# A short first chunk, its pool opened beside the image stage, residuals moved to another queue and stored in one transfer

## The chip, the cores and the metric

The kernel runs on one core of a Trainium2 chip. The core has four compute engines, TensorE (PE), VectorE (DVE), ScalarE (ACT) and GpSimd (POOL), and SyncE (SP), whose queue here only starts transfers. ACT and POOL have queues of their own from which transfers can start as well. All engines run their instructions in order and wait for one another by semaphores. The metric is the time of one execution on the device, in microseconds (us); three executions of the kernel before took 2004.09, 2007.87 and 2011.77, median 2007.87.

## The reference

The input is four images of 56 x 56 positions and 128 channels. Two layers follow each other, all in float32:

```python
# layer 0: neighbourhood attention (7x7, 4 heads), then a dense block
x = x + proj(attend(qkv(layernorm(x))))
x = x + fc2(gelu(fc1(layernorm(x))))
# layer 1, on tokens t (4, 3136, 128)
t = t + linear_attention(layernorm(t))        # q * sum_n(k * v)
t = t + stu_mixture(layernorm(t))
# stu_mixture, for each of the leading T, T/2, T/4, T/8 tokens:
#   sum over 16 filters k: irfft(rfft(phi[:, k]) * rfft(u)) @ (sigma[k]**.25 * M_phi_plus[k])
#   + the same with alternating signs and M_phi_minus
#   + three lags: u shifted by 0, 1, 2 tokens @ M_u[i]
# the mixture weights are a straight-through one-hot over the four lengths
```

The last line, the spectral filters, is the larger part of the second half of the kernel. In the frequency domain each bin has its own 128 x 128 complex matrix, made of the filters' values at this bin and of the matrices M.

## The kernel before, in words

**Image stage.** The images b = 0 to 3 are worked on one after another, each in seven groups (g) of 8 image rows = 448 tokens. An image's residual stream x lies in one of two places in SBUF, so image b + 2 is fetched into the place of image b (`fetch`, L97, on SP). For each image there is the attention (softmax on DVE, ACT and POOL: `lows`, `exps`, `shares`; L763, L777, L790), and the rest as a generator, `finish_image` (L511): the dense block, the linear attention, and the preparation of the filters. The attention of image b + 1 and `finish_image` of image b are woven together; each `yield` hands over its estimate of PE time. The whole stage, called the front, is written in manual order: every engine runs its instructions as the program text emits them. That ends with `front.close()`, which also gives the front's SBUF and PSUM space back; after it a scheduler orders the instructions.

In `finish_image` the transforms come first. For each of four slices j of the tokens, `px` (L698) multiplies tables `tab`, fetched on SP (L298), with transposed tokens `tok` (copied from PSUM by ACT, L694). The results are added by DVE and POOL into `ab`, and POOL's queue stores them as `ud[j, b]` (L722). In the last image, which has the extra pool `own`, j = 0 and 2 use `ab` and j = 1 and 3 the second buffer `ab2`.

Then, or between the slices for images 0 to 2, `last_steps` (L666) goes over the groups. `recent(g)` computes the three lags on PE (`par`, L640), and DVE adds them to x in place (L648). `residual(g - 1)` transposes the sum in four pieces on PE (`pf`, L656), ACT copies it (`xf`, L659), and SP stores it in DRAM as `xd` with four transfers, one per piece of 112 tokens, in runs of 512 B (L662). For images 0 and 1 the fetch of the same group of image b + 2 follows on SP. In images 0 to 2 xf has two buffers; in the last image it shares three buffers with `tok`.

**Matrices.** Along with the last image's `finish_image`, `matrices` (L997 to L1019) loads the M matrices on SP and combines them on DVE into `mc`. One of its steps is run for each 1 / 0.4 of yielded PE time.

**Chunk stage.** There are 245 bins, in 31 chunks (c) of 8, the last with 5. For each chunk, `tokens` fetches the spectra of all images and slices from `ud` (`xc`, L1048, 1 MB), and combines them into `v` (`evens`, L310 to L317, on POOL, for chunk 0 on DVE; `odds`, L321 to L330, and three more instructions, L1060 to L1062, on POOL). Both need scratch, `ev` and `od`, which share one buffer. `filters_of` loads `ph` for four chunks (L1070). `make(c, u)`, u = 0 to 7, computes the bins' matrices in 16 matmuls (`pg`, L1084), and DVE and ACT copy them, two copies each of 128 x 512, into `g` (L1097, L1095), which has two buffers. `product(c, part)`, eight parts, multiplies g with v (`py`, L1115); ACT and DVE combine the sums (`ya` L1128, `ys` L1132), and SP stores them in `yd` (L1134). The chunk loop runs make(c + 1, u) and product(c, u) alternately; before it, chunk 0 is made alone. All of the chunk stage's pools open after `front.close()`. For chunk 0, ph and xc are fetched on POOL's queue.

**Back transform.** After the last chunk, `ring` tiles take the sums back from `yd` in 8 transfers per parity and half on SP (`fetch_back`, L1151); butterflies on DVE (L1193, L1194) and matmuls with the table `io` (fetched on ACT, L1159) follow (`pi`, L1232); the residual xd is loaded again and added (L1244), and the result stored (L1248).

`busy(n)` issues n small matmuls whose result nobody reads.

Of the kernel before, what the change touches and what calls it, by code (L numbers as in the profile page):

```python
# [9 lines left out]
FP = mybir.dt.float32  # L10
# [15 lines left out]
GT = GR * W  # L26
QC = 14
# [22 lines left out]
NCH = -(-R // FC)  # L50
FB = 4
# [7 lines left out]
def conv_attn_hybrid_kernel(ctx: ExitStack, tc: tile.TileContext, a: dict, out: bass.AP):  # L59
# [17 lines left out]
    order = tc.manual_schedule()  # L77
    front.enter_context(order)
# [432 lines left out]
    def finish_image(b, own=None):  # L511
# [118 lines left out]
        for r in range(2):  # L630
            spread(r, f"u{b}", rs, scale)
            yield 0.25
        def recent(g):
# [3 lines left out]
            for c0, c1 in zip(cuts, cuts[1:]):  # L637
# [9 lines left out]
            xg = raster(x[:, g])  # L647
            nc.vector.tensor_tensor(  # L648
                xg, ps[:, :GT].rearrange("c (h t w) -> c h t w", h=GR, t=NQ), xg, ALU.add
            )  # L650

        def residual(g):

            pf = ps_s.tile([TQ, NQ, C], FP, tag="s", name=f"pf_{b}_{g}")
            for t in range(NQ):
                nc.tensor.transpose(pf[:, t, :], x[:, g, t * TQ : (t + 1) * TQ], ident)  # L656
            tag, bufs = ("tok", 3) if own else ("xf", 2)
            xf = fp.tile([TQ, NQ, C], FP, tag=tag, name=f"xf_{b}_{g}", bufs=bufs)
            nc.scalar.copy(xf, pf)  # L659
            rows_of = xd[b].rearrange("(g h t w) c -> g t h w c", g=NG, h=GR, t=NQ)  # L660
            for t in range(NQ):
                nc.sync.dma_start(rows_of[g, t], xf[:, t, :])  # L662
            if b + 2 < B:
                fetch(b + 2, [g])
# [12 lines left out]
        abs_of = (ab, own.tile([C, NCH, PH, 2 * FC], FP, name="ab2") if own else ab)  # L677
# [48 lines left out]
        if b == B - 1:  # L726
            yield from last_steps(range(NG))
# [265 lines left out]
    weighed = ExitStack()  # L993
    mpool = weighed.enter_context(tc.tile_pool(name="matrices", bufs=1, side="right"))
# [25 lines left out]

    with tc.tile_pool(name="last", bufs=1, side="right") as own, tc.tile_pool(
        name="weigh", bufs=1, side="right"
    ) as wp:
        extra, due = matrices(wp), 0.0
        for spent in finish_image(B - 1, own):
            due += 0.4 * (spent if spent != "step" else 0.5)
            while due >= 1:
                next(extra, None)
                due -= 1
        run(extra)  # L1030
    front.close()

    gpool = ctx.enter_context(tc.tile_pool(name="wg", bufs=2))
    with tc.tile_pool(name="w3", bufs=2) as wp, tc.tile_pool(
        name="ps_g", bufs=6, space=PSUM
    ) as ps_g, tc.tile_pool(name="ps_y", bufs=2, space=PSUM) as ps_y:
        filters_in, made, spectra, sums = {}, {}, {}, {}  # L1040
        many = [min(FC, R - FC * c) for c in range(NCH)]

        def tokens(c):


            n = NP * B
            x = wp.tile([C, n, CW], FP, tag="xc", name=f"xc{c}")
            (nc.sync if c else nc.gpsimd).dma_start(  # L1048
                x, ud.rearrange("j b c w -> c (j b) w")[:, :, CW * c : CW * (c + 1)]
            )  # L1050
            y = x.rearrange("c n (p r f) -> c p r n f", r=2, f=FC)
            v = wp.tile([C, 3, n * FC, PH], FP, tag="v", name=f"v{c}")
            w = v[:, 1:].rearrange("c r k m -> c m r k")
            gp = nc.gpsimd
            ev = wp.tile([C, 4, 2, n, FC], FP, tag="od", name=f"ev{c}", bufs=1)
            evens(gp if c else nc.vector, ev, y[:, :4], w[:, :4])
            od = wp.tile([C, 3, 2, 2, n, FC], FP, tag="od", name=f"od{c}", bufs=1)
            odds(gp, od, y[:, 4:])
            od = od.rearrange("c i p r n f -> c i p r (n f)")
            gp.tensor_tensor(w[:, 4:6], od[:, 0], od[:, 2], ALU.add)  # L1060
            gp.tensor_tensor(w[:, 6:], od[:, 0], od[:, 2], ALU.subtract)
            gp.tensor_scalar(v[:, 0], v[:, 2], -1.0, 1.0, ALU.mult, ALU.mult)  # L1062
            spectra[c] = v

        def filters_of(k):

            t = wp.tile([C, FB * CW], FP, tag="ph", name=f"ph{k}")
            n = min(FB, NCH - FB * k) * CW
            for rg in range(4):
                (nc.scalar if k else nc.gpsimd).dma_start(  # L1070
                    t[32 * rg : 32 * rg + 32, :n], pd[:, FB * CW * k : FB * CW * k + n]
                )
            filters_in[k] = t

        def make(c, u):

            if u == 0:
                made[c] = gpool.tile([C, CW, C], FP, tag="g", name=f"g{c}")
            g, t, at = made[c], filters_in[c // FB], c % FB * CW
            banks = [ps_g.tile([C, 4, CW], FP, tag="g", name=f"pg_{c}_{u}_{i}") for i in range(4)]  # L1080
            for q in range(4):
                for rg in range(4):
                    r = slice(32 * rg, 32 * rg + 32)
                    nc.tensor.matmul(  # L1084
                        banks[rg][:, q, :],
                        mc[r, 4 * u + q, :],
                        t[r, at : at + CW],
                        start=True,
                        stop=True,
                    )  # L1090
            for rg in range(4):
                into = g[:, :, 32 * rg + 4 * u : 32 * rg + 4 * u + 4]
                src = banks[rg].rearrange("c q n -> c n q")
                if rg % 2:
                    nc.scalar.copy(into, src)  # L1095
                else:
                    nc.vector.tensor_copy(into, src)  # L1097

        def weights(v, r, f, m):

            return v[:, r : r + 2].rearrange("c r (n f) m -> c f m (r n)", f=FC)[:, f, m]

        def product(c, part):

            v, g = spectra[c], made[c]
            f0 = part // 4 * 4
            h, last = part // 2 % 2, min(many[c], f0 + 4)
            if part % 2 == 0:
                sums[0] = ps_y.tile([C, 4, C], FP, tag="y", name=f"py_{c}_{part}")
            py, f1 = sums[0], f0 + part % 2 * 2  # L1110
            for f in range(f1, min(f1 + 2, last)):
                for r in range(2):
                    for m in range(4):
                        slot = SLOTS.index(4 * h + m)
                        nc.tensor.matmul(  # L1115
                            py[32 * m : 32 * m + 32, f - f0, :],
                            weights(v, 1 - r, f, slot),
                            g[:, (2 * slot + r) * FC + f, :],
                            start=(r == 0),
                            stop=(r == 1),  # L1120
                        )
            if part % 2 == 0:
                return

            k = last - f0
            if h == 0:
                sums[1] = wp.tile([C, 4, C], FP, tag="ya", name=f"ya_{c}_{part}", bufs=1)
                nc.scalar.copy(sums[1][:, :k], py[:, :k])  # L1128
                return
            for i, op in enumerate((ALU.add, ALU.subtract)):  # L1130
                ys = wp.tile([C, 4, C], FP, tag=f"ys{i}", name=f"ys_{c}_{part}_{i}")
                nc.vector.tensor_tensor(ys[:, :k], sums[1][:, :k], py[:, :k], op)  # L1132
                at = FC * c + f0
                nc.sync.dma_start(yd[i, at : at + k, :C].rearrange("f q e -> q f e"), ys[:, :k])  # L1134

        ring, ready, waves_back = [], {}, {}
        PAIR = 2 * B * C

        def ring_tile():
            name = f"ring{len(ring)}"
            ring.append(gpool.tile([C, 2, 4, 2, PAIR], FP, tag="g", name=name))

        def fetch_back(pair, par, fh):
            y = ring[fh][:, 1 - par]

            for m in range(4):
                for r in range(2):
                    row = 16 * (2 * m + r) + 8 * pair  # L1150
                    nc.sync.dma_start(  # L1151
                        y[:, m, r],
                        yd[par, RT[fh] : RT[fh] + C, row : row + 8].rearrange("f n e -> f (n e)"),
                    )
            return y.rearrange("f m s (j x) -> f j m s x", j=2)

        def odd_waves(pool, pair, fh):
            t = pool.tile([C, 32 * L], FP, tag="io", name=f"io_{pair}_{fh}")
            nc.scalar.dma_start(t, a["itab_odd"][pair, fh])  # L1159
            return t.rearrange("f (j k m r p n) -> f j k m r p n", j=2, k=2, m=2, r=2, p=2)  # L1160

        filters_of(0)
# [257 lines left out]
```

## Time and profile before

| | |
|---|---|
| median of three executions | 2007.87 us |
| profiled execution | 2007.11 us, of which span 2005.3 |
| PE busy, mean granted clock | 1870.1 us (93%), 0.96 |
| DVE, ACT, POOL busy | 1201.7, 1029.5, 904.8 us |
| image stage up to the last slices | 0 to 1083 us |
| last image's dense block and transforms | 1083 to 1241 us |
| passage to the chunks | 1241 to 1287 us |
| chunk loop | 1287 to 1803 us |
| back transform | 1803 to 2005 us |
| mean DMA rate over the span | 110 GB/s of HBM traffic |

In the lines of the profile, L1084 is line 1084 of the kernel before, `pg<-ph,mc` means that pg is written from ph and mc, and `A <- B: 9.2, 6, 2.9` that instruction group A waited 9.2 us in total for B, 6 times, longest 2.9. In the table of stages the columns are: stretch and its length, busy time (and number of instructions) of PE, of PE's weight loads, of DVE, ACT and POOL, then PE's granted clock as a share of full speed, the busy share of the 16 DMA engines, and GB/s. In the chain, every line is a start, a duration and the work that held up the next. SPq is the time that SP's queue took to issue a transfer. A name with DMA in front is a transfer's time after its issue.

### The profile page before, as it was taken

How to read it: one execution, taken by the hardware profiler on the slowest of the kernel's cores; microseconds unless marked ns; L12 is line 12 of the kernel's file. 1: busy time of each engine (PE TensorE's matmuls, PEld its weight loads, DVE VectorE, ACT ScalarE, POOL GpSimd, SP SyncE). 2: the span in 40 equal slices, each digit the busy share in tenths (PEclk: the TensorE clock that was granted, in tenths of full speed). 3: DMA queues.
4: the chain of work that ended last, by engine and by line, in shares of the span. 5: the costliest groups of instructions: out<-in, count | busy, mean ns of one | idle time of the engine just before them, and what ended most of it. 6: DMA issues, size and time to landing. Idle time of an engine off the chain costs nothing.

```text
span 2005.3 us, 57209 instructions
## 1 busy us (share of the span) xinstructions
PE 1870.1 (93%) x23914; PEld 1196.6 (60%) x23914; DVE 1201.7 (60%) x2749; ACT 1029.5 (51%) x2311; POOL 904.8 (45%) x1446
## 2 busy tenths in 40 slices
PE   6899999998999998999998989799999999996998
PEld 3555555554555554555555445688888888882333
DVE  2676645454645554545556674577777777775883
ACT  1566685654685654685655433355555555550000
POOL 2344322464321563322564026588877777770000
PEclk8799999898999998999999989799999999997999
DMA  4040000053000063000154538444444444439991
GB/s 114 31 133 12 1 1 1 28 197 129 1 1 1 28 212 113 1 1 1 54 184 158 181 96 280 112 135 130 134 130 125 119 130 133 128 88 373 369 329 65
DMA packets 191391, 223.45 MB, mean 111 GB/s; under 512 B 12008, under 2 KB 171049, under 8 KB 188540
## 3 DMA queue, kind: packets, MB, share of 16 engines
q1 hardware_dynamic: 182992, 166.69, 27.1%
q0 software_dynamic: 2752, 34.33, 4.4%
q10 hardware_dynamic: 5388, 18.76, 2.6%
q8 instruction: 189, 3.10, 0.6%
q14 instruction: 70, 0.57, 0.1%
HBM read 141.77 MB, written 77.97 MB: 110 GB/s over the span
## 4 chain that ended last, share of the span: by engine, by line
PE 74%; issue 7%; DVE 5%; DMA 5%; ACT 4%; POOL 2%; SPq 2%; ACTq 0%; DVEq 0%; POOLq 0%
PE pg L1084 14%; PE py L1115 13%; PE pi L1232 7%; PE px L698 4%; PE ppt L806 4%; PE pl L750 3%; PE ph L549 3%; PE pf L540 3%; PE par L640 2%; PE pav L863 2%; PE pv L826 2%; DMA ring<-yd 2%; PE pk L481 2%; SPq L662 2%; DVE p L763 1%
## 5 line engine op out<-in xcount | busy, mean ns | idle before, releaser
L790 POOL TENSOR_SCALAR p<-p,den 112x280 f32<-112x280 f32 x448 | 216.1, 502 | 497.7 <-DVE den L788 265.5
L1097 DVE COPY g<-pg 128x512 f32<-128x512 f32 x496 | 319.8, 688 | 156.4 <-PE pg L1084 147.4
L1095 ACT COPY g<-pg 128x512 f32<-128x512 f32 x496 | 271.1, 602 | 234.1 <-PE pg L1084 226.7
L1084 PE MATMUL pg<-ph,mc 32*128 32x128 f32 x7936 | 297.0, 286 | 10.7 <-ACT g L1095 4.1
L1084 PEld LDWEIGHTS pg<-ph,mc 32*128 32x128 f32 x7936 | 249.7, 189 | 51.1 <-issue 39.1
L777 ACT ACTIVATE p<-p,low 112x280 f32<-112x280 f32 x448 | 231.1, 517 | 93.8 <-DVE low L763 93.5
L1115 PE MATMUL py<-g,v 128*32 128x128 f32 x7840 | 274.8, 281 | 2.6 <-issue 1.1
L1115 PEld LDWEIGHTS py<-g,v 128*32 128x32 f32 x7840 | 218.8, 152 | 32.2 <-issue 3.2
L763 DVE CUSTOM_DVE_ANT_0 p<-pl,bias 112x280 f32<-112x280 f32 x448 | 174.7, 445 | 15.6 <-PE pl L750 3.5
L698 PE MATMUL px<-tab,tok 98*128 98x496 f32 x256 | 122.0, 618 | 18.4 <-DMA tab<-in_tab 9.2
L813 DVE COPY pt<-ppt 120x448 f32<-120x448 f32 x112 | 69.4, 620 | 110.8 <-PE ppt L806 109.9
L806 PEld LDWEIGHTS ppt<-ident,p 112*120 112x120 f32 x896 | 100.4, 139 | 58.0 <-issue 41.5
L806 PE MATMUL ppt<-ident,p 112*120 112x112 f32 x896 | 127.0, 263 | 5.2 <-DVE middle L848 3.9
L1232 PE MATMUL pi<-ring,io 128*98 128x512 f32 x256 | 113.2, 603 | 17.2 <-DVE ring L1194 16.2
L706 POOL TENSOR_TENSOR ab<-ab,w 128x496 f32<-128x496 f32 x60 | 74.1, 1235 | 104.6 <-ACT w L705 87.0
L813 ACT COPY pt<-ppt 120x448 f32<-120x448 f32 x224 | 87.2, 444 | 53.9 <-PE ppt L806 53.6
L750 PE MATMUL pl<-kt,qt 32*112 32x280 f32 x896 | 94.8, 442 | 11.5 <-ACT qt L500 6.0
L549 PE MATMUL ph<-ln_m,w_fc 128*128 128x448 f32 x224 | 102.7, 550 | 3.0 <-DVE ln_m L530 3.0
L540 PE MATMUL pf<-h,w_fc 128*128 128x448 f32 x224 | 100.8, 540 | 0.0
L557 ACT ACTIVATE h<-ph,b_fc 128x448 f32<-128x448 f32 x112 | 69.4, 634 | 58.7 <-PE ph L549 57.1
L1232 PEld LDWEIGHTS pi<-ring,io 128*98 128x98 f32 x256 | 42.7, 168 | 87.0 <-issue 82.1
L698 PEld LDWEIGHTS px<-tab,tok 98*128 98x128 f32 x256 | 48.1, 200 | 74.6 <-issue 46.1
(239 smaller groups left out, 3294.5 us busy)
## 6 DMA issues: line engine op xcount, KB each, us to landing
ring<-yd SPq DMA_DIRECT2D x64, 512.0 KB
ud<-ab POOLq DMA_DIRECT2D x16, 1984.0 KB, 7.4
yd<-ys SPq DMA_DIRECT2D x122, 256.0 KB
xc<-ud SPq DMA_DIRECT2D x30, 1024.0 KB
tab<-in_tab SPq DMA_DIRECT2D x160, 189.9 KB
mat<-in_M_phi_plus SPq DMA_DIRECT2D x16, 512.0 KB
mat<-in_M_phi_minus SPq DMA_DIRECT2D x16, 512.0 KB
x<-in_x SPq DMA_DIRECT2D x28, 224.0 KB
```

Source lines behind the costliest of these rows:

```text
L540: nc.tensor.matmul(po[:, :GT], late["w_fc2"][:, i, :], hts[g - 1][i], start=(i == 0), stop=(i == 3),)
L549: nc.tensor.matmul(ph[:, :GT], w_fc1[:, i * C : (i + 1) * C], lnm[:, g * GT : (g + 1) * GT], start=True, stop=True,)
L698: nc.tensor.matmul(ps, toks[i // 4][:, i % 4, :], next(tab), start=True, stop=True)
L763: nc.vector.tensor_tensor_reduce(out=f["p"][:, h, :], in0=f["pls"][h][:TQ, :KEYS], in1=bias[:, h, :], scale=-1.0, scalar=3.0e38, op0=ALU.a ...
L777: nc.scalar.activation(f["p"][:, h, :], f["p"][:, h, :], AF.Exp, bias=f["low"][:, h : h + 1], scale=-1.0, accum_out=f["den"][:, h : h + 1],)
L790: nc.gpsimd.tensor_scalar(f["p"][:, h, :], f["p"][:, h, :], f["den"][:, h : h + 1], 1.0, ALU.mult, ALU.mult)
L806: nc.tensor.transpose(ppt[:, i, :], of, ident[:TQ, :TQ])
L1084: nc.tensor.matmul(banks[rg][:, q, :], mc[r, 4 * u + q, :], t[r, at : at + CW], start=True, stop=True,)
L1095: nc.scalar.copy(into, src)
L1097: nc.vector.tensor_copy(into, src)
L1115: nc.tensor.matmul(py[32 * m : 32 * m + 32, f - f0, :], weights(v, 1 - r, f, slot), g[:, (2 * slot + r) * FC + f, :], start=(r == 0), stop ...
L1232: nc.tensor.matmul(banks[j, p], it, z, start=(fh == 0 and k == 0), stop=(fh == 1 and k == len(of) - 1),)
```

## The change

1. The residual's sum goes into a new tile `xr` in place of x. Transposes take every fourth token, so that a partition holds four neighbouring tokens and one transfer with runs of 2 KB stores a group; it is issued on ACT. In the last image xf lies in the places of the chunk sums `ys0` and `ys1`.
2. In the last image `ab2` is used for j = 0 and 2 and `ab` for 1 and 3.
3. The matrices are paced at 0.45 instead of 0.4.
4. `finish_image` says when the last image's spectra are done. Then `own` and `weigh` close, the chunk pool opens beside the front, and chunk 0's ph (SP) and xc (SP, in two parts) are fetched before the last steps. `tokens(0)` stands in the manual order two steps before their end, with evens on DVE and odds on POOL in buffers of their own. `busy(6)` follows. make(0) is written in manual order too; the scheduler starts after it.
5. Chunk 0 has 5 bins and all others 8. In chunk 0 the copies of g, the products and the stores leave out the first SKIP = 3 bins; the input table is shifted to match.
6. The two buffers of g become two pools. `mc` is kept to the end, and the first half of the table `io` is loaded into its place.
7. The last chunk's sums are stored on ACT's queue, the others on SP's as before.

```diff
@@ finish_image
-            xg = raster(x[:, g])
-            nc.vector.tensor_tensor(
-                xg, ps[:, :GT].rearrange("c (h t w) -> c h t w", h=GR, t=NQ), xg, ALU.add
+            xr[g] = temp(f"xr_{b}_{g}")
+            nc.vector.tensor_tensor(
+                xr[g].rearrange("c (h t w) -> c h t w", h=GR, t=NQ),
+                ps[:, :GT].rearrange("c (h t w) -> c h t w", h=GR, t=NQ),
+                raster(x[:, g]),
+                ALU.add,
             )
@@ residual
-            pf = ps_s.tile([TQ, NQ, C], FP, tag="s", name=f"pf_{b}_{g}")
-            for t in range(NQ):
-                nc.tensor.transpose(pf[:, t, :], x[:, g, t * TQ : (t + 1) * TQ], ident)
-            tag, bufs = ("tok", 3) if own else ("xf", 2)
-            xf = fp.tile([TQ, NQ, C], FP, tag=tag, name=f"xf_{b}_{g}", bufs=bufs)
+            pf = ps_s.tile([TP, XQ, C], FP, tag="s", name=f"pf_{b}_{g}")
+            for t in range(XQ):
+                nc.tensor.transpose(pf[:, t, :], xr[g][:, t::XQ], ident)
+            if own:
+                xf = cp.tile([TP, XQ, C], FP, tag=f"ys{g % 2}", name=f"xf_{b}_{g}")
+            else:
+                xf = fp.tile([TP, XQ, C], FP, tag="xf", name=f"xf_{b}_{g}", bufs=2)
             nc.scalar.copy(xf, pf)
-            rows_of = xd[b].rearrange("(g h t w) c -> g t h w c", g=NG, h=GR, t=NQ)
-            for t in range(NQ):
-                nc.sync.dma_start(rows_of[g, t], xf[:, t, :])
+            nc.scalar.dma_start(
+                xd[b, g * GT : (g + 1) * GT].rearrange("(n t) c -> n t c", t=XQ), xf
+            )
@@ transforms
-        abs_of = (ab, own.tile([C, NCH, PH, 2 * FC], FP, name="ab2") if own else ab)
+        abs_of = (own.tile([C, NCH, PH, 2 * FC], FP, name="ab2") if own else ab, ab)
         if b == B - 1:
+            yield "spectra"
             yield from last_steps(range(NG))
@@ chunk stage
+    def fetch_tokens(c):
+        n = NP * B
+        x = cp.tile([C, n, CW], FP, tag="xc", name=f"xc{c}")
+        src = ud.rearrange("j b c w -> c (j b) w")[:, :, CW * c : CW * (c + 1)]
+        for part in (slice(n),) if c else (slice(n - B), slice(n - B, n)):
+            nc.sync.dma_start(x[:, part], src[:, part])
+        fetched[c] = x
     def tokens(c):
-            ev = wp.tile([C, 4, 2, n, FC], FP, tag="od", name=f"ev{c}", bufs=1)
-            evens(gp if c else nc.vector, ev, y[:, :4], w[:, :4])
-            od = wp.tile([C, 3, 2, 2, n, FC], FP, tag="od", name=f"od{c}", bufs=1)
+        of, tag, bufs = [C, 3, 2, 2, n, FC], *(("od", 1) if c else ("v", 2))
+        if c == 0:
+            od = cp.tile(of, FP, tag=tag, name=f"od{c}", bufs=bufs)
...
+        evens(gp if c else nc.vector, ev, y[:, :4], w[:, :4])
+        if c:
+            od = cp.tile(of, FP, tag=tag, name=f"od{c}", bufs=bufs)
         odds(gp, od, y[:, 4:])
     def make(c, u):
+            if c == 0:
+                into, src = (
+                    z.rearrange("c (x f) q -> c x f q", f=FC)[:, :, SKIP:] for z in (into, src)
+                )
     def product(c, part):
-                nc.sync.dma_start(yd[i, at : at + k, :C].rearrange("f q e -> q f e"), ys[:, :k])
+            (nc.scalar if c == NCH - 1 else nc.sync).dma_start(
+                yd[i, at + skip : at + 4, :C].rearrange("f q e -> q f e"), ys[:, skip:]
+            )
@@ order of the passage
-        extra, due = matrices(wp), 0.0
-        for spent in finish_image(B - 1, own):
-            due += 0.4 * (spent if spent != "step" else 0.5)
+        extra, due, last = matrices(wp), 0.0, finish_image(B - 1, own)
+        for spent in last:
+            if spent == "spectra":
+                break
+            due += 0.45 * (spent if spent != "step" else 0.5)
             while due >= 1:
                 next(extra, None)
                 due -= 1
         run(extra)
+    cp = chunks.enter_context(tc.tile_pool(name="w3", bufs=2, side="right"))
+    filters_of(0)
+    fetch_tokens(0)
+    for n, _ in enumerate(last):
+        if n == 2 * NG - 3:
+            tokens(0)
+    busy(6)
     front.close()
-    gpool = ctx.enter_context(tc.tile_pool(name="wg", bufs=2))
+    gpools = [ctx.enter_context(tc.tile_pool(name=f"wg{i}", bufs=1)) for i in range(2)]
+    for u in range(8):
+        make(0, u)
+    order.close()
```

## The prediction

> **What bounds the kernel now.** I read the page's busy shares first, then a table of stages cut where the work changes, then for each stage the list of waits and the chain of work that ended last.
>
> ```profile
> core 0: us, PE busy (x) PEld busy (x) DVE busy (x) ACT busy (x) POOL busy (x), PEclk, DMA share, GB/s
> 0.00:1083.00 1083.00, 1004.52 (x7242) 584.22 (x7243) 572.85 (x1866) 655.28 (x1638) 436.37 (x822) 0.96 0.19 61
> ...
> 1241.00:1263.00 22.00, 15.02 (x66) 9.62 (x64) 7.08 (x12) 4.00 (x7) 5.00 (x10) 0.90 0.82 251
> 1263.00:1271.00 8.00, 3.88 (x50) 3.58 (x50) 0.91 (x2) 0.74 (x2) 7.75 (x11) 0.50 0.45 116
> 1271.00:1287.00 16.00, 12.95 (x268) 11.47 (x272) 10.22 (x17) 8.65 (x17) 14.99 (x22) 0.75 0.40 109
> 1287.00:1803.00 516.00, 516.00 (x15312) 448.74 (x15304) 374.41 (x597) 295.67 (x539) 399.63 (x547) 1.00 0.43 122
> ...
> 1812.00:1860.00 48.00, 31.80 (x68) 11.74 (x68) 32.22 (x29) 0.00 (x0) 0.00 (x0) 0.79 0.97 382
> ```
>
> TensorE (PE) bounds nearly everything, and completely the 516 us of the chunk loop, where it never idles at a clock of 1.00. What a schedule can still win is PE's idle time and its slow clock elsewhere: 78.5 us in the image stage, 14.1 us from 1241 to 1287 plus what half clock costs there, and 16.2 us around 1812 to 1860, where the DMA share is 0.97. The change works on all three. The middle one, the passage from the last image to the chunks, has these waits:
>
> ```profile
> POOL od L321 <- DVE v L317: 10.4, 1, 10.4
> DVE g L1097 <- DMA xd<-xf: 9.0, 1, 9.0
> ...
> POOL ph L1070 <- DMA xd<-xf: 7.6, 1, 7.6
> ACT g L1095 <- DMA xd<-xf: 7.4, 1, 7.4
> ...
> PE pg L1084 <- ACT g L1095: 4.1, 1, 4.1
> PE pg L1084 <- issue: 3.5, 1, 3.5
> PE pf L656 <- DVE x L648: 3.5, 1, 3.5
> ```
>
> The three PE lines add to 11.1 us. The chain of the same stretch says who is behind them:
>
> ```profile
> 1248.75 3.68 DMA xd<-xf
> ...
> 1258.87 3.34 DMA xd<-xf
> 1262.31 0.59 ACT xf L659
> ...
> 1267.16 2.41 DMA xd<-xf
> ...
> 1270.26 0.59 ACT g L1095
> 1270.90 3.44 PE pg L1084 x40
> ```
>
> SyncE's queue issues the 28 residual stores of the last image one by one (0.63 us each); the xf buffers, and afterwards the front's space into which g is copied, come free only when these have landed. In the image stage the same queue shows:
>
> ```profile
> PE px L698 <- DMA tab<-in_tab: 9.2, 6, 2.9
> ...
> PE xm_a L388 <- DMA x<-in_x: 5.8, 4, 2.2
> ...
> PE px L698 <- ACT tok L694: 5.6, 11, 1.1
> ```
>
> **The change, part by part.** The sum is made against the profiled execution, 2007.1 us (span 2005.3 and 1.8 around it), 0.8 under the median 2007.9.
>
> *Passage to the chunks.* The last image's 28 store issues on SP become 7 on ACT; the waits for their landing go, and POOL's fetch of ph and xc behind them; ev leaves the place ahead of x_6 on DVE. The last transposes pf_6 then follow the add of group 6 as in the other groups (2.69 us from one group to the next): the 3.5 us go, and the first pg, which needs ACT's last xf to free its bank, starts about 1257.5 instead of 1262.99 (xf no longer waits 3.66 for a store: four buffers, and a store is 4 periods = 10.8 us old when its place is wanted, against 3.7 us of landing). The fillers of busy(6) lie in that gap. From there make(0) has eight u. Before, the first 40 records took until 1270.9 (waits 4.1, half clock 0.50); then a u took 1.74 us, of which 1.17 was PE and 0.57 a wait for DVE's two copies (0.688 each). A copy of 320 elements instead of 512 I estimate at 0.48 on DVE and 0.43 on ACT, from the rows of 128x128 (0.29, 0.27) and 128x512 (0.69, 0.60). Two of them fall below PE's 1.10 to 1.17, so a u costs 1.2 at full clock; I take 1.5, since the first u's may still run slow. 1257.5 + 8 x 1.5 = 1269.5; add 0.7 for evens standing ahead of the first copies: first product at about 1270.2 against 1286.25, **-16** (bounds: -17.8 with 1.2 a u and no stall up front, -13 if the first four u's run at half clock and wait as before). That needs v0 by then: xc0 was issued at 1249.60 and landed about 1257.1; on POOL odds and the three instructions after them took 8.5 us (1261.2 to 1269.7); now odds start when xc0 lands, beside evens on DVE, and end about 1265.6. Cover left: 4 us. If ud's last slice (issued 1239.47, 7.4 us to land) or xc0 comes later than that, the product moves back one for one.
>
> A rule that speaks against this split: the Trainium skill, "SBUF — State Buffer", section "Who interferes with whom", says that a VectorE instruction with two inputs in SBUF and a GpSimd instruction that reads SBUF exclude one another. This trace has both kinds only apart here, though one GpSimd add of the image stage ran 2112 ns where the median is 1132. By the rule the evens (4 us) and odds would run in turn, v0 come 4 us later, and the cover just be used up: the sum would stay at -16 to -15.
>
> *First chunk short.* make(0) is in the above. product(0) issues 160 records instead of 256 and product(30) 256 instead of 160; at 33 ns a record (1.05 per 32) 3.2 us leave the front and arrive at the end. At the end they lie before the gap of 16.22 us in which PE waits for the returned sums anyway, and would hide if the last sums' stores were not late by as much. I take **-2** (0 to -3.2).
>
> *End of the chunks.* The chain here is loads at full DMA:
>
> ```profile
> 1803.25 8.42 DMA ring<-yd
> ...
> 1811.69 9.55 DMA ring<-yd
> ...
> 1826.42 7.93 DMA yd<-ys
> ...
> 1834.92 8.34 DMA ring<-yd
> ```
>
> PE waits 16.22 us for the butterflies behind the first two of these lines. The table io (1.48 MB) was issued at 1802.26 and took 93% of the DMA time to 1808, ahead of the sums. Its issue is now ahead of the last g copies, about 2.5 us earlier: -2.5. The four last stores (1 MB) leave SP's queue, where they sat until 1823.87, for ACT's, where they run beside the first ring loads. At the stage's 382 GB/s 1 MB is 2.7 us: +1.3 (shared with loads) to +2.7. Their landing ended the wait of ring1's loads until 1834.4, so the second half comes earlier, and 0.9 of PE's idle before it with it. Together **-2** (-4 to +2).
>
> *Matrices at 0.45 instead of 0.4.* Before, four matrix loads stood behind the ten tables in SP's queue and two matrix operations (1.27) ahead of reciprocals on the softmax path; of the wait of 10.9 on DVE only 1.1 reached PE. **-2** (-1 to -3: the rows 1.1, 0.4, 1.1).
>
> *Residuals of images 0 to 2.* 84 stores on SP become 21 on ACT, of 2 KB runs instead of 512 B. SP gains: a group of four took 2.7 to 5.4 us in front of tab and x loads. The waits of 9.2 and 5.8 can all go (-15); I count two thirds, -10, because some will meet the next limit, ACT's tok, which already holds px 5.6. The new xr adds the same work on DVE (one two-input add), frees x before pf instead of after, and costs nothing by itself; the transposes now read every fourth column, and the strided weights of py load in 152 ns against 189 for the contiguous ones of pg, so I add nothing there either (twice their 0.27 us would be +23 if none of it lay beside other work, which no row suggests). ACT pays: an issue on its queue has taken 0.33 to 0.39; with the wait for its own copy to finish I say 0.55 x 21 = 11.6 us, with ACT busy 0.60 of this stage. Queued behind each are tok copies, softmax exponentials and pt copies, for which PE waits. Nothing of it on the path gives 0, all of it +11.6; I take +5. **-5** (-12 to +4).
>
> Sum: -16 -2 -2 -2 -5 = -27, **1980**; all terms at their ends together give -40 and -8, 1967 and 1999.
>
> The skill's "DMA: Bandwidth & Descriptors", section "Issuing engines are not separate DMA queues", says that another issuing engine saves only sequencer time. By it the attention term would be the issue time of SP that PE sees and the end term +2.7 without relief, in sum about 1985; no run here has yet shown it.
>
> **Rivals.**
> 1. *The passage is stalled by something new.* ACT's queue now holds the loads of ph1 and the seven stores, and each waits for its predecessors; v0 needs all of ud. For it: 0.82 DMA share in 1241 to 1263, before a single moved transfer. Against: cover of 4 us. Then the first product is at 1278 to 1282 and the loop starts only 4 to 8 us earlier; with the next three terms as they are and the images at half, -6 -2 -2 -2 -2.5 = -14.5: about 1992.
> 2. *Nothing gained in the images.* The waits for tables are replaced by waits for ACT. For it: 11 waits on tok. The term is 0 to +5: 1985 to 1990, say 1987.
> 3. *ACT's issues block it, and the kernel gets slower.* ACT executes in order; if a store's issue on it waits for an earlier store's landing (3.6 us each, from 10.9 in 3 waits of "ACT xf <- DMA xd<-xf" before), 21 x 3.6 = 76 us stand ahead of softmax work. With the other gains at -22, it turns the sign from 1.05 us an issue on the path, and exceeds 0.5% from 1.5 us; at 2 us it is +42 - 22 = +20: 2027. Against: in images 0 to 2 two xf buffers never waited for a store.
>
> **How the numbers follow.** Forecast 0.58 (1968 to 1988), rival 1 0.15, rival 2 0.17, rival 3 0.10. A measurement here tells about 0.5%, 10 us: under 1997.8 is faster. The forecast and rival 2 lie there wholly, rival 1 for the larger part (0.08): 0.83. Same 0.09, from the rest of rival 1 and a mild rival 3; slower 0.08. The range goes to 1968 below (two terms at their best) and to 2003 above, which takes in rival 1 with the tail's loss added and leaves out rival 3.
>
> **What the changed profile would show.** Right: first py near 1260 to 1266 on its own clock (1270 less the 7 gained earlier); no wait of DVE g on xd stores; no PEclk of 0.5 over 8 us; PE without a wait on tab longer than 1 us; pi's wait before its first record at 13 to 16 us. Wrong: ACT's sequencer waiting for xd landings, a py wait on POOL's v, or PE's waits on ACT tok well above 5.6. The forecast falls if the image stage takes over 1083 us, or the passage over 36 us from par of group 0 to the first py.

## The result and the profile after

The changed kernel takes 2003.48 us in the median of 13 executions against 2008.03 for the kernel before in 13, a ratio of 0.9975 with a 95% interval of 0.9957 to 0.9992. The forecast was 1980, with a range of 1968 to 2003; a gain of 27 was announced and 5 came, with the median just outside the range. The profiled execution (2011.3 us, span 2009.5) is the slowest of the 13; it is used below to see where time went, and the medians for how much.

The start and end records of the matmul groups in the trace cut both spans into five stretches. The last column is the changed kernel with 38 small matmuls put at its very start, which the experiments will explain.

| stretch, us | before | after | after, 38 small matmuls |
|---|---|---|---|
| start to the end of par (image stage) | 1254.5 | 1245.2 | 1232.9 |
| end of par to first py (passage) | 31.8 | 20.7 | 19.5 |
| first py to end of the last pg (chunk loop) | 515.9 | **540.6** | 513.6 |
| end of the last pg to first pi | 25.2 | 24.9 | 24.4 |
| first pi to the end | 178.0 | 178.1 | 177.8 |
| span | 2005.3 | 2009.5 | 1968.2 |

The stretches that the change was to shorten did get shorter, by 9.3 and 11.1 us in these two profiles. The chunk loop, of which nothing but the first and last round was touched, got 24.7 us longer and ate it. (In the changed kernel ten u of make lie ahead of the first py where nine did, since the first product of the short chunk 0 is empty; so the border between passage and loop stands one u, 1.5 us, later in the work.) The table of stages of the changed kernel (columns as before):

```profile
1230.00:1251.00 21.00, 18.93 (x122) 13.62 (x120) 8.86 (x14) 4.86 (x9) 7.32 (x11) 1.00 0.99 307
1251.00:1266.00 15.00, 12.04 (x288) 10.29 (x292) 8.04 (x18) 6.55 (x17) 14.69 (x21) 0.89 0.30 79
...
1600.00:1700.00 100.00, 96.48 (x2764) 82.83 (x2760) 68.18 (x109) 52.67 (x98) 72.96 (x101) 1.00 0.42 114
...
1817.00:1864.00 47.00, 30.56 (x75) 11.47 (x68) 27.89 (x22) 0.00 (x0) 0.00 (x0) 0.82 1.03 404
```

Half clock has nearly gone from the passage: the clock's records have 3.4 us of it (1251.3 to 1254.7), where the kernel before had 20.5 (1258.4 to 1278.9). But in the loop TensorE, which had been busy 516 of 516 us, is now idle 3.5 of 100. The waits of the passage, of the image stage and of the loop, in this order:

```profile
PE pg L1088 <- DVE g L1106: 5.2, 9, 1.8
PE pf L663 <- DVE xr L652: 0.3, 1, 0.3
```

```profile
PE px L708 <- ACT tok L704: 8.2, 10, 1.6
```

```profile
PE py L1124 <- issue: 10.6, 18, 1.0
```

In the passage 5.2 us of waits for g are left of 11.1 (0.6 of them just behind the first py), and no copy of g waits for xd any more. In the image stage the waits for tables (9.2) and images (5.8) are gone, and the one for ACT's tok has grown from 5.6 to 8.2. The third is new: py waits 18 times for "issue", that is for nothing that any semaphore shows. A wait counts there only from the modelled end of the last matmul, 0.27 us after its start, where matmuls otherwise start every 0.033 us; so each stop is longer than listed, short stops are not listed at all, and 10.6 us listed are compatible with 24.7 lost.

One chunk of the loop shows the stop and what lies beside it. First TensorE's timeline, then SyncE's:

```profile
1654.49 0.77 PE L1124 MATMUL py<-g,v 128*32 128x128 f32 x17
1656.18 0.69 PE L1124 MATMUL py<-g,v 128*32 128x128 f32 x15 [0.92 <-issue]
```

```profile
1648.48 0.36 SPq L1042 DMA_DIRECT2D xc<-ud  x1
```

The stop follows the issue of xc, the 1 MB load for a later chunk, by 7 us, in chunk after chunk. The DMA view of the stretch 1647.4 to 1653.6, in which the load comes to fill the engines (two stores of yd, issued at 1652.16, follow it):

```profile
DMA  0000000000000134436999999999999999999999
...
q1 hardware_dynamic: 2162, 1.10, 66.3%
```

and of the next 1.4 us:

```profile
q1 hardware_dynamic: 861, 0.43, 105.7%
q8 instruction: 1, 0.02, 5.3%
```

Queue q8 carries instructions, in packets of 16 KB. The page of the kernel before had it too, in a line that I passed over:

```profile
q8 instruction: 189, 3.10, 0.6%
```

189 blocks of 16 KB are 3.10 MB, or 65 bytes for each of TensorE's 2 x 23914 recorded instructions; I take 64 bytes, so 256 instructions a block. A chunk has 512 weight loads and 512 matmuls in the trace, so four blocks, one every 4.3 us. In the changed kernel none is fetched between 1646.3 and 1653.7; TensorE runs out at about 1655.

### The profile page after: what moved, and what is told of

Its sections match the earlier page's. It is cut to its first block, busy times and chain, and to the rows that moved or that the text cites. A ratio compares the mean times of both kernels' runs of the same rounds, so it can differ in the third digit from the quotient of the medians.

```text
span 2009.5 us, 57128 instructions
## 1 busy us (share of the span) xinstructions
PE 1881.9 (94%) x23926; PEld 1206.8 (60%) x23926; DVE 1204.3 (60%) x2749; ACT 1024.2 (51%) x2311; POOL 904.1 (45%) x1441
## 4 chain that ended last, share of the span: by engine, by line
PE 77%; issue 8%; DVE 6%; DMA 4%; ACT 3%; POOL 2%; ACTq 0%; SPq 0%; DVEq 0%; POOLq 0%
PE pg L1088 14%; PE py L1124 13%; PE pi L1272 7%; PE px L708 5%; PE ppt L817 4%; PE pl L761 4%; PE ph L551 3%; PE pf L542 3%; PE par L644 3%; PE pav L874 2%; PE pv L837 2%; PE pk L483 2%; ACT p L788 1%; DVE p L774 1%; DMA ud<-ab 1%
## 5 line engine op out<-in xcount | busy, mean ns | idle before, releaser
L1106 DVE COPY g<-pg 128x512 f32<-128x512 f32 (+1 forms) x496 | 320.3, 691 | 171.2 <-PE pg L1088 171.1
L1104 ACT COPY g<-pg 128x512 f32<-128x512 f32 (+1 forms) x496 | 263.9, 584 | 236.8 <-PE pg L1088 236.8
L1124 PE MATMUL py<-g,v 128*32 128x128 f32 x7840 | 283.0, 281 | 12.6 <-issue 12.2
L1124 PEld LDWEIGHTS py<-g,v 128*32 128x32 f32 x7840 | 222.5, 152 | 46.8 <-issue 18.1
L774 DVE CUSTOM_DVE_ANT_0 p<-pl,bias 112x280 f32<-112x280 f32 x448 | 174.8, 446 | 15.9 <-PE pl L761 4.1
L708 PE MATMUL px<-tab,tok 98*128 98x496 f32 x256 | 118.1, 607 | 12.6 <-ACT tok L704 9.8
L318 POOL TENSOR_TENSOR v<-ev 128x512 f32<-128x512 f32 x30 | 39.6, 1320 | 120.1 <-PE py L1124 120.0
L564 DVE SCALAR_TENSOR_TENSOR x<-pf,b_fc,x 128x448 f32<-128x448 f32 x28 | 19.1, 684 | 113.0 <-PE pf L542 113.0
```

The source lines that it names most:

```text
L708: nc.tensor.matmul(ps, toks[i // 4][:, i % 4, :], next(tab), start=True, stop=True)
L774: nc.vector.tensor_tensor_reduce(out=f["p"][:, h, :], in0=f["pls"][h][:TQ, :KEYS], in1=bias[:, h, :], scale=-1.0, scalar=3.0e38, op0=ALU.a ...
L1124: nc.tensor.matmul(py[32 * m : 32 * m + 32, f - f0, :], weights(v, 1 - r, f, slot), g[:, (2 * slot + r) * FC + f, :], start=(r == 0), stop ...
```

## Experiments

**1. Moving the fetches against the loads.** The theory is that a block asked for while xc's packets hold the DMA engines comes late, and that the change moved the blocks' borders relative to the chunks: the short first chunk takes 48 matmuls out of the front of the loop, each four TensorE instructions here (two weight loads, two matmuls), so 192 instructions or three quarters of a block. The rival is that something in the new chunk stage itself, its pools or its order, is slower. Small matmuls that nobody reads, put where TensorE waits for its first weights anyway, move the borders and touch nothing else (up to 64 of them leave the first steps behind them where they were, fold_qkv at 11.13 us; 102 put them 3.1 us later):

```diff
     nc.gpsimd.memset(eps, EPS)
+    blank = cpool.tile([32, 32], FP, name="blank")
+    nc.vector.memset(blank, 0.0)
+    unread = bank("unread")
+    for _ in range(38):
+        nc.tensor.matmul(unread[:32, :32], blank, blank, start=True, stop=True)
```

> The changed kernel with 38 matmuls of 32x32 at the very start, where TensorE waits 6.5 us for its first weights; nothing else differs. Each float32 matmul is four TensorE instructions here, so the stream of TensorE instructions before the chunk loop is 152 longer. Theory (instruction fetch): TensorE's instructions arrive in blocks of 16 KB = 256 instructions, four blocks a chunk; in the changed kernel one of the four is asked for while the 1 MB load xc holds the DMA engines, comes 2 to 3 us late, and TensorE stands 0.3 to 1.0 us in each chunk. 152 instructions move the fetches by 2.6 us against xc, out of the load's way: chunk period back from 18.3 to 17.26 us, no wait of py for 'issue', some 25 us less than the changed kernel, about 1978. Rival (the loop is slower because of the two single-buffer pools of g, of the right-hand chunk pool, or the last stores): the loop stays at 18.3 us a chunk and the time at about 2003.

> Control: the changed kernel with 64 such matmuls at the start, 256 instructions, one whole block. Instruction fetch: the blocks fall as in the changed kernel, chunk period stays about 18.3 us, time about 2003. Rival (the small matmuls at the start help or harm by themselves, through the clock or the first banks): the time moves as in the run with 38.

> The kernel before with 24 such matmuls at the start, 96 instructions. Instruction fetch: the fetches move 1.6 us earlier against xc, where the changed kernel has them; the loop gets TensorE waits on 'issue', chunk period from 17.26 to about 18.2 us, time 2008 + 25 = about 2033. Rival (something else in the changed chunk stage): the time stays at 2008.

> The changed kernel with 8 of the small matmuls at the start (32 instructions): the fetches move 0.54 us earlier against xc. Instruction fetch: the block that was due 2.6 us after xc's issue and came at 4.9 is now due at about 2.1 and still comes at 4.9, so TensorE stands 0.5 us longer in each of some 27 chunks: +15 on the changed kernel, about 2018. Rival (38 matmuls helped by something that grows with their number): a fifth of the gain, about 1998.

> The changed kernel with 19 of them (76 instructions), fetches 1.3 us earlier: the block is due about 1.3 us after xc's issue, just before the load's packets fill the DMA engines (from about 1.5). If it gets in ahead of them, no chunk loses anything: about 1978. If it is still caught, this is the worst place, +1.3 us a chunk: about 2035. Rival as above: half of the gain, about 1989.

> The changed kernel with 102 small matmuls at the start: 38 and one whole block of 256 instructions. Instruction fetch is periodic in 64 matmuls: as with 38, a loop without waits and about 1977 (the longer row of small matmuls may delay the start by some us). Without the period: no better than with 64, 2004.

| kernel | small matmuls | median, us | ratio to before, 95% interval | loop in the profile, us |
|---|---|---|---|---|
| before | 0 | 2008.0 | 1 | 515.9 |
| before | 24 | 2037.5 | 1.0139 (1.0113 to 1.0165) | 547.7 |
| after | 0 | 2003.5 | 0.9975 (0.9957 to 0.9992) | 540.6 |
| after | 8 | 2007.9 | 0.9984 (0.9960 to 1.0007) | 544.4 |
| after | 19 | 1990.2 | 0.9895 (0.9862 to 0.9928) | 532.1 |
| after | 38 | 1975.3 | 0.9823 (0.9798 to 0.9848) | 513.6 |
| after | 64 | 2004.0 | 0.9976 (0.9957 to 0.9995) | 541.7 |
| after | 102 = 38 + 64 | 1981.2 | 0.9864 (0.9837 to 0.9890) | 513.0 |

Each ratio is taken against the kernel before as it ran beside that kernel (medians 2008.0 to 2010.1 us).

The kernel before can be made 28 us slower and the changed one 28 us faster by instructions at the start that do nothing, and a whole block of them (64 matmuls) changes nothing: not from 0 to 64, and from 38 to 102 not in the loop (of the 6 us between these two medians 3.1 are the later start, the rest is not resolved). The rival falls: with the borders elsewhere the new chunk stage runs its loop in 513 us. The other rival, a gain that grows with the number of small matmuls, named 1989 for 19 and is met there by 1990.2, but 8, 64 and 102 contradict it. The waits of TensorE in the loop with 38 matmuls, then with 64, then those of the kernel before with 24:

```profile
PE pg L1093 <- DVE g L1111: 0.6, 1, 0.6
```

```profile
PE py L1129 <- issue: 16.4, 20, 1.2
```

```profile
PE py L1120 <- issue: 18.5, 24, 1.2
```

The packets of q8 in the records say when the blocks of one chunk were fetched, in us from the issue of its xc:

| kernel, xc issued at | fetches | stop of TensorE | to the next xc |
|---|---|---|---|
| before, 1653.75 | -0.4, 5.1, 8.7, 12.8 | none | 17.26 |
| after, 1648.48 | -2.2, 5.2, 8.9, 12.5 | 0.92 at 6.8 | 18.62 |
| after with 38, 1599.43 | -0.4, 5.2, 9.0, 12.9 | none | 17.27 |
| after with 64, 1609.50 | -1.9, 5.0, 8.8, 12.3 | 0.91 at 6.7 | 18.55 |
| after with 8, 1505.38 | -2.1, 5.4, 9.1, 12.6 | 1.66 at 6.4 | 19.18 |
| after with 19, 1278.95 | -2.0, 3.8, 7.5, 11.0 | 0.42 at 6.0 | 18.08 |
| after with 19, 1712.47 | -2.8, 0.8, 5.8, 9.8 | none | 17.23 |

A block wants to come every 4.3 us. In the kernel before, in the changed one, and in those with 24, 38, 64 and 102, the one due inside the load's 1.5 to 5 us is held until the load is nearly through: none starts between 1 and 4 us after the issue. With 8 and 19 this is not so in every chunk: in 10 and 11 of 27 a block starts 2.5 to 4 us after it, though the load fills the engines there too. Where two fetches lie 5.5 us apart there is no stop, at 7.4 us there is one of 0.9 and the chunk takes 1.3 us longer; between 5.2 and 6.2 both were seen (5.9 with 19: a stop of 0.42). Over all chunks of the loop, the longest distance between two fetches around a load, and the time of a chunk:

| kernel | distance, us: median, most | median us a chunk |
|---|---|---|
| before | 5.2, 5.9 | 17.26 |
| after with 38 | 5.2, 5.7 | 17.27 |
| after | 6.7, 7.4 | 18.34 |
| after with 64 | 6.8, 7.4 | 18.41 |
| before with 24 | 6.9, 7.8 | 18.56 |

My numbers for 8 and 19 were too simple: I let the held block come at 4.9 whatever its due time. With 8 it gets in earlier in the later chunks, so that 4 us were lost instead of 15. With 19 the two cases that I had set against each other both occur: the blocks stop TensorE in most of the early chunks, and from about 1610 on get in ahead of the load. The borders drift against the chunks: in the kernel before the fetch next to the issue moves from 0.0 us at the start of the loop to -0.6 at its end. Probably a chunk has an instruction or two more than four blocks; the trace does not list them.

**2. Which part of the change moved the borders.** The changed kernel with its fifth part undone:

```diff
-            if c == 0:
-                into, src = (... [:, :, SKIP:] for z in (into, src))
...
-        h, skip = part // 2 % 2, max(SKIP - f0, 0) if c == 0 else 0
+        h, last = part // 2 % 2, min(R - FC * c, f0 + 4)
...
-    full[..., SKIP:] = tab
+    full[..., :R] = tab
```

> The changed kernel with its fifth part undone: all of chunk 0's 8 bins, and the last chunk short as before; no small matmuls. 48 matmuls = 192 TensorE instructions move from the end to the front of the loop. Instruction fetch: the fetches move 3.2 us earlier against xc, into the place they had before (due about 3.6 us after xc's issue, when the load is nearly over): loop without waits on 'issue', about 1978 to 1980, i.e. 1975 and some 2 to 5 for the 512-element copies in make(0) and the longer first product. If the short first chunk as such were harmless and the loop slow for another reason: about 2003 plus 2.

Measured: 1986.27 us, ratio 0.9894 (0.9864 to 0.9924). The waits for issue fall to 1.3 us:

```profile
PE py L1119 <- issue: 1.3, 2, 1.0
```

The loop takes 524.8 us instead of 540.6, although its first round is longer; in a middle chunk the fetches lie at -0.5 and 4.9, in the late ones at -0.8 and 5.3 with 17.5 to 18.1 us a chunk, so this place is at the edge and some loss remains. The short first chunk by itself, meant to save 2 us, thus cost 17 in the medians. The expected 1978 to 1980 was missed by 6 to 8 us; the loop, with the same work in it as before, is 8.9 us longer than before (515.9), which is enough for that.

**3. The residuals alone.** On the kernel before; TensorE's instructions are as many as before, and the loop keeps its 17.27 us a chunk. (Only the store's lines are shown; the sum in xr and the transposes of every fourth token go with them.)

```diff
-            nc.scalar.copy(xf, pf)
-            rows_of = xd[b].rearrange("(g h t w) c -> g t h w c", g=NG, h=GR, t=NQ)
-            for t in range(NQ):
-                nc.sync.dma_start(rows_of[g, t], xf[:, t, :])
+            nc.scalar.copy(xf, pf)
+            nc.scalar.dma_start(
+                xd[b, g * GT : (g + 1) * GT].rearrange("(n t) c -> n t c", t=XQ), xf
+            )
```

> The kernel before with the change to the residuals alone: the sum in xr, transposes of every fourth column, one transfer per group on ACT's queue, buffers of xf as before. TensorE's instructions are as many as before, so the fetches stay where they were. Prediction's terms: images 0 to 2 -5 (between -12 and +4), and in the passage the waits for 28 stores on SP mostly go, some -8: about 1995. If the stores on ACT cost what they save (rival 2): 2000. If ACT is blocked by landings (rival 3): above 2008.

The second run has `nc.sync` in the place of `nc.scalar` in the last lines:

> The kernel before with the change to the residuals alone, but the one store per group on SP, where the four were, not on ACT (1986.5 with ACT). If the number of issues was the price (0.64 us each on SP), most of the gain stays: about 1989. If the price was that SP stands waiting for xf in front of the loads of tables and images, most of the image stage's gain goes: about 2000.

Measured: 1986.51 with ACT's queue, ratio 0.9882 (0.9861 to 0.9903); 1991.82 with SP's, 0.9901 (0.9873 to 0.9930). The intervals overlap: four fifths or all of the gain comes from one transfer in the place of four, and the queue is not resolved. The waits of the image stage with ACT's queue, first TensorE's, then ACT's:

```profile
PE px L704 <- ACT tok L700: 8.2, 10, 1.6
```

```profile
ACT xf L665 <- DMA xd<-xf: 2.1, 1, 2.1
...
ACT tok L700 <- ACT xf L665: 1.2, 3, 0.4
```

and of TensorE with the store on SP:

```profile
PE px L704 <- ACT tok L700: 5.6, 11, 1.1
PE xm_a L389 <- DMA x<-in_x: 2.9, 2, 1.7
PE px L704 <- DMA tab<-in_tab: 1.0, 1, 1.0
```

What SP's queue waits for in front of these stores, before and with one store on SP:

```profile
SPq L662 <- ACT xf L659: 89.3, 9, 15.6
...
SPq L662 <- ACT tok L694: 32.9, 4, 10.9
```

```profile
SPq L666 <- ACT xf L665: 122.3, 17, 13.0
```

SP stands in front of its stores for 122 us as it did before, yet the loads behind them are late for 3.9 us in place of 15.0. So it was the four issues, 0.64 us each, more than the standing. Fewer issues and longer runs (2 KB for 512 B) came together here and were not tried apart. With ACT's queue both waits are gone and ACT pays little: one wait of 2.1 us for a landing in 21 stores, and tok makes TensorE wait 2.6 us more. The Trainium skill, "DMA: Bandwidth & Descriptors", section "Issuing engines are not separate DMA queues", holds that moving the issue to another engine saves no more than issuing time; that two runs with different queues cannot be told apart agrees with it.

**4. Evens of chunk 0 on GpSimd.** On the changed kernel with 38 small matmuls:

```diff
-        evens(gp if c else nc.vector, ev, y[:, :4], w[:, :4])
+        evens(gp, ev, y[:, :4], w[:, :4])
```

> The changed kernel with 38 small matmuls (1975.3), and chunk 0's evens on GpSimd as in every other chunk, not on VectorE beside the odds. In the profile v0 was ready 8.5 us before the first product, and TensorE waited 1.9 us for VectorE's first copies of g, which stood behind evens. Expected: that wait goes, v0 comes 2 to 3 us later and is still early: from the last par to the first py 17.6 instead of 19.5 us, time -1.9, about 1973. If the split pays (v0 late on GpSimd alone): TensorE waits for v before the first py, time above 1975.

Measured: 1981.0, ratio 0.9839 (0.9812 to 0.9867), not to be told from 0.9823. The waits of the passage with the split and without it:

```profile
PE pg L1093 <- DVE g L1111: 5.6, 10, 1.9
```

```profile
PE pg L1093 <- DVE g L1111: 4.2, 10, 0.6
...
PE py L1129 <- issue: 1.0, 1, 1.0
```

The wait of 1.9 us for the first copies goes, as expected, and TensorE does not wait for v; from the last par to the first py it takes 18.2 instead of 19.5 us, 1.4 less by the waits for g where 1.9 were expected. (The wait for issue lies in the loop, at 1275.) What the split cost is seen in the timeline with it, VectorE's evens and GpSimd's odds:

```profile
1233.60 1.17 POOL L333 TENSOR_TENSOR od<-xc 128x256 f32<-128x256 f32 x1
...
1234.10 0.94 DVE L318 TENSOR_TENSOR ev<-xc 128x256 f32<-128x256 f32 x1
...
1234.97 0.54 DVE L319 TENSOR_TENSOR ev<-xc 128x128 f32<-128x128 f32 x1
```

Alone, in the kernel before, the same evens took 0.41 and 0.28 us. Beside the odds they take 0.94 and 0.54, and an odd of 0.71 takes 1.17.

The time did not follow. The profiled execution is even 13.3 us longer (1983.34 against 1970.01), but 12.5 of these lie ahead of the edit: up to the end of px the two programs are the same, but one got there at 1214.4 and the other at 1226.9. From 340 us to about there (columns as in the tables of stages), with the split and without:

```profile
340.00:1213.00 873.00, 827.78 (x5285) 471.69 (x5284) 484.99 (x1326) 516.26 (x1206) 357.78 (x582) 0.97 0.27 92
```

```profile
340.00:1225.00 885.00, 838.89 (x5282) 476.45 (x5281) 483.90 (x1324) 516.67 (x1206) 357.30 (x582) 0.96 0.27 90
```

The same instructions keep TensorE busy for 11.1 us more, with the granted clock a little lower; the clock's records have 51 us at half speed between 330 us and the end of the image stage in the one and 79 in the other. The single executions of one kernel spread by 10 to 20 us, and this is a part of it; a gain of 1 or 2 us cannot be seen in so few of them.

**5. The pace of the matrices.**

```diff
-            due += 0.45 * (spent if spent != "step" else 0.5)
+            due += 0.4 * (spent if spent != "step" else 0.5)
```

> The changed kernel with 38 small matmuls, the matrices at a pace of 0.4 as before instead of 0.45. By the prediction's term: +2 (1 to 3), about 1977, and the wait on the last matrix in the last image's transforms comes back. If the pace did nothing: 1975.

Measured: 1979.28, ratio 0.9851 (0.9821 to 0.9880), 4 us more, with overlapping intervals. The waits of the last image's transforms and gates, with 0.4:

```profile
PE rb_u L445 <- DVE ln_u L635: 2.5, 1, 2.5
PE px L713 <- DVE ab L735: 1.7, 1, 1.7
...
PE px L713 <- DVE ab L731: 1.0, 1, 1.0
```

With 0.45:

```profile
PE ph L556 <- DVE ln_m L537: 1.7, 1, 1.7
PE px L713 <- DVE ab L735: 1.6, 1, 1.6
...
PE rb_u L445 <- DVE ln_u L635: 0.5, 1, 0.5
```

The three waits are 0.5, 1.6 and none, 3.1 us less, but ph now waits 1.7 us for VectorE's ln_m, as it does for 1.6 or 1.7 us in the other profiles with 0.45 and not with 0.4. That leaves 1.4 us, within the forecast term, and the time does not resolve it.

**6. The last sums' stores.**

```diff
-            (nc.scalar if c == NCH - 1 else nc.sync).dma_start(
+            nc.sync.dma_start(
```

> The changed kernel with 38 small matmuls, the last chunk's four stores back on SP behind the first ring loads. By the prediction's end term, of which the relief of the stores is about half: +1, and the second half of pi waits 0.9 us again; if the stores beside the ring loads only cost (1.3 to 2.7): the stretch from the last pg to the first pi gets that much shorter and the time is 1973 to 1974.

Measured: 1973.77, ratio 0.9831 (0.9803 to 0.9858), not resolved from 0.9823. From the last pg to the first pi it takes 22.3 instead of 24.4 us; the nine profiles of the changed kernel and its variants with these stores on ACT have 24.4 to 26.3. SP's issues with the stores on ACT, then on SP:

```profile
1769.36 17.55 SPq L1168 DMA_DIRECT2D ring<-yd  x12
```

```profile
1768.97 14.43 SPq L1168 DMA_DIRECT2D ring<-yd  x15
```

With the stores on ACT's queue the first ring loads are issued later: the records show SP's issues at 5.5, 7.2, 7.9, 11.5 and 15.9 us after the last pg, where without them ten lie between 5.4 and 13.7. SP's queue, from 1766 to 1800 with the stores on ACT:

```profile
SPq L1168 <- DMA yd<-ys: 6.2, 3, 4.0
```

Of these 6.2 us 4.4 lie before 1783, in the first half's loads, and with the stores on SP there is none there. So by the profile the second alternative fits: beside the ring loads the stores only cost. By the time alone it is open.

## Why the prediction was wrong

- **The step that failed** is the part "First chunk short". It counted the 48 matmuls (96 records) moved from the front to the end by their duration, 3.2 us, and took nothing else of them. By duration they are a small matter, as was said: with the borders out of the way the loop is 2.3 us shorter than before, with 128 records fewer in it (4.2 us at 33 ns each: the 96, and the 32 of the u that moved ahead of the first py). What was left out is that these matmuls are also 192 instructions of TensorE's stream, three quarters of a fetched block, and that everything behind them keeps the new phase: 25 us over the loop. None of the three rivals had it. All three looked for the loss in the passage or the images, the only stretches with visible idle time; the loop stood as "never idle", which was true and did not say that it had little slack. The signs of being right did appear (first py at 1265.9, no copy of g waiting for xd, half clock for 3.4 us); none of them looked at the loop. That the time ended half a microsecond from the range's upper end is chance: this end was made of rival 1, which did not occur.
- **Images 0 to 2**, -5: the mechanism was right, the size too small. Both kinds of wait went, as the term's far end allowed (-15 for the waits), and ACT's price, taken as +5, was 2.6 us of tok. The residuals alone gave 23 us in the medians, of which 4.9 lie in the passage by the profile, so some 18 in the images; the lower bound of -12 was too narrow. That waits also cost half clock behind them may explain the rest: from 330 us to the end of par the records have 78.5 us at half clock before and 68.3 with the residuals changed. But they differ by more than that between executions (51 and 79 in experiment 4), so it is not shown.
- **Passage**, -16: 12.2 with the 38 matmuls, 11.1 without. First pg 2.6 us after par, as forecast (1257.5 less 1254.5 is 3.0), and a u took 1.54 against 1.5. Two terms were mis-sized: the loop makes a u of chunk 1 ahead of each product, and the first product of the short chunk 0 is empty, so ten u lie before the first py and not eight (3.1 us); and the evens ahead of the first copies cost 1.9, not 0.7, since they ran slowly beside the odds. The sign named for a failing passage, over 36 us from par of group 0 to the first py, did appear: 39.4 (38.2 with 38). Two slips in the working did no harm: eight u at 1.2 give 1267.1, so the far bound is -19.2 (-18.5 with the evens), not -17.8; and 48 records, not 40, ran before the wait that ended at 1270.9. The cover for v0 was larger than thought, with 38 8.5 us by the timeline, not 4: xc0 had landed by 1231, before the last par.
- **The rule weighed there**, from the Trainium skill, "SBUF — State Buffer", section "Who interferes with whom", agrees in kind with the evens at 0.94 and 0.54 us beside the odds, 0.41 and 0.28 alone. I let it make v0 late, which it did not; it made VectorE late for g.
- **End**, -2: 0.8 to the first pi. With the stores on SP it is 2.9 (25.2 to 22.3), for which the earlier table is the named reason, though no run isolates it; the stores on ACT gave 2.1 of it back. No relief of the second half is seen: from the first pi to the end it takes 177.8 us with 38, against 178.0 before.
- **Pace**, -2: about -1.4 by the waits, unresolved by the time.
- **Rival 1** did not occur: no wait of TensorE or of the copies of g on xd, ud or v is left in the passage. **Rival 2** is contradicted by experiment 3. **Rival 3**: ACT waited for a landing once, for 2.1 us.
- Without the loss the sum was too cautious: 1975.3 with 38 small matmuls, against 1980 forecast.

## What to carry to other kernels

Where an engine runs a stream of small instructions without a pause, the stream itself has to be fetched, and it shares the DMA engines with the kernel's loads. Look for the instruction queue in the page's DMA part, divide its bytes by the loop's length, and ask where the large loads stand against it; any change in the number of instructions ahead of the loop moves that phase, so compare two versions of a kernel at more than one phase (a few idle matmuls at the start are enough) before the difference is put down to the edit. Four small stores on a queue that also carries loads cost more than their bytes: put them into one transfer first, and choose the queue afterwards.

## What the runs showed of the hardware

- TensorE's instructions are fetched in blocks of 16 KB, here one every 4.3 us of the loop. A 1 MB load held a due block back by some 3 us (due at 2.1, come at 5.2 us from the issue), and two fetches 7.4 us apart stopped TensorE for about 1 us; 5.5 us apart did not. The Trainium skill, "Runtime: NRT & Kernel Launch", section "Instruction fetch mechanics", describes the blocks of 256 instructions and calls the cost of a border mostly hidden. These runs agree on the size and differ on the cost: 25 to 32 us, up to 1.6% of the kernel, by the phase alone. Why the block waits for the load is not shown, nor why it does not always: with 8 and 19 small matmuls some packets of q8 started while the load filled the engines, 0.4 to 1.7 us after they were due.
- Such a stop appears as a wait for "issue" without a releaser, and in part not at all, since it begins under the modelled end of the last matmul.
- Of two programs that are the same up to the end of px, one execution had 51 us at half clock between 330 us and there and the other 79, and was 12.5 us behind at the end of par.
